# Mixing channels on four quarters of TensorE's array, and laying one stage's work between another's by time

## The chip, the cores and the metric

The kernel runs on one core of one Trainium2 chip. The metric is the device time of one execution in microseconds; the time of the kernel before is the median of three runs. All data are fp32. The engines are called as in the profile: PE is TensorE's matmul, PEld its weight load, DVE is VectorE, ACT is ScalarE, POOL is GpSimd, and SP is the queue that issues the transfers.

## The reference, cut to what matters

Four layers follow each other on a tensor of 4 images x 64 channels x 256 x 256. Layers 0, 2 and 3 are long convolutions in two dimensions with a separable filter, plus a bias times the input. Layer 1 works on Haar coefficients:

```python
def _L1_conv_ref(x, v, conv_w, tau):          # x: (4, 64, 256, 256)
    f1 = haar2d(x)
    acc = jnp.zeros_like(f1[:, :conv_w.shape[1]])
    for i in range(v.shape[0]):               # two terms, i = 0 and 1
        f3 = f1 * v[i]
        f4 = jnp.einsum('bchw,oc->bohw', f3, conv_w[i])      # mixes the 64 channels
        f5 = jnp.sign(f4) * jax.nn.relu(jnp.abs(f4) - tau[i])
        acc = acc + f5
    y = haar2d(acc, inverse=True)
    return y + x
# ... layers 0, 2, 3:  y = (2D convolution of x with hx * hy) + x * bias
```

v[i] and tau[i] have one value per pixel, and v is the same for all channels, so the kernel mixes first and multiplies by v afterwards.

## The kernel before

The batch is cut into two groups of two images. The kernel has three phases. A is layer 0 and the Haar transform, and writes the coefficients to DRAM (`coef`). B is the mixing of channels and the threshold, and writes `mixed`. C is the inverse transform with layers 2 and 3. B is laid beside the others: B of the first group beside A of the second, and B of the second group beside C. Each phase is a list of pieces, and `beside` says how many pieces of the one follow each piece of the other; an engine works through its instructions in the order in which the pieces emit them.

A round of A treats two channels of two images, and has 12 pieces: four of rows, four of columns and four of the product with the Haar matrix (M = 4). A round of C has 16.

```python
    def toeplitz(ps, data, t, which):                      # a row or column piece: 2 x this pair
        for m in range(2):
            cut = bass.ts(m, P)
            nc.tensor.matmul(ps[:, m, :], data[:, 0, cut], t[:, which, :], start=True, stop=False)
            nc.tensor.matmul(ps[:, m, HALF:], data[:, 1, cut], t[:, which, :HALF], start=False, stop=True)
# ... phase A, column piece: what VectorE does after it
            later(
                lambda: nc.vector.scalar_tensor_tensor(
                    s["x1"][:, cut], s["x"][:, cut], bias_sb[:, c : c + 1], ps, ALU.mult, ALU.add
                )
            )
# ... phase A, product piece
            for e in range(2):
                for k in range(2):
                    nc.tensor.matmul(
                        ps[:, e, bass.ts(k, P)],
                        s["fw"][:, 2 * (n + e) + k, bass.ts(m, P)],
                        haarH_sb[:, k, :],
                        start=True,
                        stop=True,
                    )
```

Phase B goes by rows of coefficients, 64 steps of two units each (P = 128, C = 64, N = 256, W = 512, NB = 2). In the first group ("not packed") 64 channels x 2 rows fill the partitions, and a unit is one of the two terms i. In the second group ("packed") a unit is one image, and the matrix holds both terms side by side: its 128 output columns are 64 channels of term 0 and 64 of term 1. The lower 64 partitions of the data hold one row, the upper 64 another; each half of the array's rows mixes its own.

```python
        def mix(u):
            f = st[u // 2]["f"]
            un[u]["f4"] = bps.tile([P, 2, W], F32, tag="f4", name=f"f4_{grp}_{u}")   # PSUM, two buffers
            if packed:
                for h in range(2):
                    cut = bass.ts(h, N)
                    for q in range(2):
                        rows = slice(q * C, (q + 1) * C)
                        nc.tensor.matmul(
                            un[u]["f4"][:, q, cut],
                            mixers[0][rows, 0],
                            f[rows, u % 2, cut],
                            start=True,
                            stop=True,
                            tile_position=(q * C, 0),
                        )
            else:
                for j in range(2):
                    nc.tensor.matmul(un[u]["f4"][:, j, :], mixers[0][:, u % 2, :], f[:, j, :], start=True, stop=True)
        def multiply(u):
            f4 = un[u]["f4"]
            nc.vector.tensor_tensor(f4, f4, weights(u, "v"), ALU.mult)
        # sign(u):      m  = sign(f4)              ScalarE
        # magnitude(u): f4 = abs(f4)               ScalarE
        # less(u):      f4 = f4 - tau              VectorE
        def threshold(u):
            nc.vector.scalar_tensor_tensor(un[u]["m"], un[u]["f4"], 0.0, un[u]["m"], ALU.max, ALU.mult)
# ...
        def sort(s, name, q):                              # packed only
            if q == 0:
                tag, bufs = ("gt", 3) if name == "g" else ("other", 2)
                st[s][name] = bp.tile([P, NB, W], F32, tag=tag, name=f"{tag}_{grp}_{s}", bufs=bufs)
            i = q if name == "g" else 1 - q
            src = st[s]["m"][i * C : (i + 1) * C, :, q]
            nc.scalar.copy(st[s][name][q * C : (q + 1) * C], src)

        def add_sorted(s, name):
            g = st[s]["g"]
            nc.gpsimd.tensor_tensor(g, g, st[s][name], ALU.add)
# ...
        def unit(u, j):
            if j == 0:
                if u < units:
                    mix(u)
                if 0 < u <= units:
                    less(u - 1)
            elif j == 1:
                if u < units:
                    multiply(u)
                    sign(u)
                if 0 < u <= units:
                    threshold(u - 1)
            elif u < units:
                magnitude(u)
```

In the packed result the partitions stand for the term and the free dimension for the row, while the output needs the row on the partitions and the sum of both terms. So four copies per step (`sort`) bring the parts to their places, into `g` and `other`, and two additions on GpSimd add the input and `other`.

```python

    def beside(main, side, lead, tail):

        done = 0
        for k, p in enumerate(main):
            p()
            want = len(side) * max(0, k + 1 - lead) // max(1, len(main) - lead - tail)
            for q in side[done:want]:
                q()
            done = max(done, want)
# ...
    beside(a[cut_a : -6 * M], phase_b(0, False), 5 * M, 0)       # A of group two, B of group one
# ...
    beside(main, phase_b(1, True), 5 * M, 0)                     # C, B of group two
```

Of the kernel before, what the change touches and what calls it, by code (L numbers as in the profile page):

```python
# [35 lines left out]
F32 = mybir.dt.float32  # L39
AF = mybir.ActivationFunctionType  # L40
ALU = mybir.AluOpType
# [3 lines left out]
P = 128  # L45
B, C, N = 4, 64, 256
# [10 lines left out]
COPIES = 8  # L57

GROUPS = 2
NB = B // GROUPS  # L60
CI = 4 // NB
M = CI * NB

ROUNDS = C // CI
STEPS = C
W = 2 * N
# [10 lines left out]
def conv_haar_kernel(  # L77
    ctx: ExitStack, tc: tile.TileContext, x, zT, w1, wbd, cols, decay, wo_first, decay_first, bias, haarW, haarH, ident, wcol, wrow, mixT, packT, v, v2, tau, out
):
    nc = tc.nc  # L80
# [11 lines left out]
    taus2 = dram.tile([C, 2, COPIES, 2, W], F32, tag="taus2", name="taus2")  # L92


    def pool(name, bufs, stack=ctx, **kw):
        return stack.enter_context(tc.tile_pool(name=name, bufs=bufs, reuse_waits="tile", **kw))
# [151 lines left out]
    def copy_tau(k):  # L248
        tau_sb = thresholds[1]
        for i in range(2):  # L250
            at = taus2.offset + (i * COPIES + k) * 2 * W
            to = bass.AP(taus2.tensor, at, [[4 * W * COPIES, C], [W, 2], [1, W]])
            nc.sync.dma_start(to, tau_sb[:, 2 * i : 2 * i + 2].rearrange("p h k -> p (h k)"))

    first_x = [load_x(0)]
# [19 lines left out]
    rest += [lambda l=l, q=q, k=k: spread(l, q, k) for l in (1, 2) for q in range(4) for k in thirds]  # L275
    rest.append(scale_tau)
    rest += [lambda k=k: copy_tau(k) for k in range(COPIES)]

    def toeplitz(ps, data, t, which):
# [238 lines left out]
    def phase_b(grp, packed):  # L518
# [3 lines left out]
        mixers = []  # L522
        st = [dict() for _ in range(STEPS)]
        un = [dict() for _ in range(units)]
        pieces = []

        def rows_of(ap, s):
            n = NB * W
            by_partition = [[n, P]] if packed else [[n, C], [C * n, 2]]
            return bass.AP(ap.tensor, ap.offset + 2 * s * C * n, by_partition + [[1, n]])  # L530

        def load(s):
            if s >= STEPS:
                return
            d = st[s]
            d["f"] = bp.tile([P, NB, W], F32, tag="ft", name=f"ft_{grp}_{s}", bufs=4)
            nc.sync.dma_start(d["f"].rearrange("p b w -> p (b w)"), rows_of(coef[grp], s))
            for name, src in (("v", v2), ("tau", taus2)) if packed else (("v", v), ("tau", taus)):
                t = d[name] = bp.tile([P, 2, W], F32, tag=name, name=f"{name}_{grp}_{s}", bufs=3)
                if packed:  # L540

                    at, by_partition = s * 4 * W * COPIES, [[2 * W, 2 * COPIES], [0, C // COPIES]]
                else:

                    at, by_partition = s * 4 * W, [[0, C], [2 * W, 2]]
                flat = bass.AP(src.tensor, src.offset + at, by_partition + [[1, 2 * W]])
                nc.sync.dma_start(t.rearrange("p e w -> p (e w)"), flat)
# [5 lines left out]
        def mix(u):  # L553
            f = st[u // 2]["f"]
            un[u]["f4"] = bps.tile([P, 2, W], F32, tag="f4", name=f"f4_{grp}_{u}")
            if packed:

                for h in range(2):
                    cut = bass.ts(h, N)
                    for q in range(2):  # L560
                        rows = slice(q * C, (q + 1) * C)
                        nc.tensor.matmul(  # L562
                            un[u]["f4"][:, q, cut],
                            mixers[0][rows, 0],
                            f[rows, u % 2, cut],
                            start=True,
                            stop=True,
                            tile_position=(q * C, 0),
                        )
            else:  # L570

                for j in range(2):
                    nc.tensor.matmul(un[u]["f4"][:, j, :], mixers[0][:, u % 2, :], f[:, j, :], start=True, stop=True)  # L573
# [29 lines left out]
                st[s]["g"] = bp.tile([P, NB, W], F32, tag="gt", name=f"gt_{grp}_{s}", bufs=3)  # L603
                nc.gpsimd.tensor_tensor(st[s]["g"], m0, un[2 * s + 1]["m"], ALU.add)

        def sort(s, name, q):

            if q == 0:
                tag, bufs = ("gt", 3) if name == "g" else ("other", 2)
                st[s][name] = bp.tile([P, NB, W], F32, tag=tag, name=f"{tag}_{grp}_{s}", bufs=bufs)  # L610
            i = q if name == "g" else 1 - q
            src = st[s]["m"][i * C : (i + 1) * C, :, q]
            nc.scalar.copy(st[s][name][q * C : (q + 1) * C], src)  # L613

        def add_sorted(s, name):
            g = st[s]["g"]
            nc.gpsimd.tensor_tensor(g, g, st[s][name], ALU.add)  # L617

        def store(s):
            nc.sync.dma_start(rows_of(mixed[grp], s), st[s]["g"].rearrange("p b w -> p (b w)"))  # L620
            st[s].clear()
# [15 lines that stand above are left out]
# [10 lines left out]
        def piece_packed(u, j):  # L647
            unit(u, j)
            s, i = divmod(u, 2)

            if j != 1:
                of = s - 1 if (i, j) != (0, 0) else s - 2
                name, q = {(0, 2): ("g", 0), (1, 0): ("g", 1), (1, 2): ("other", 0), (0, 0): ("other", 1)}[i, j]
                if 0 <= of < STEPS:
                    sort(of, name, q)
            if j == 1 and i and 1 <= s <= STEPS:
                add_sorted(s - 1, "f")
            if j == 1 and not i and 2 <= s <= STEPS + 1:
                add_sorted(s - 2, "other")
                store(s - 2)  # L660
            if j == 1 and not i and s >= 2:
                load(s + 2)

        def start():
# [183 lines left out]
        pieces.append(lambda: (flush(), store(total - 1)))  # L848
        return before, first, pieces

    def beside(main, side, lead, tail):

        done = 0
        for k, p in enumerate(main):
            p()
            want = len(side) * max(0, k + 1 - lead) // max(1, len(main) - lead - tail)
            for q in side[done:want]:
                q()
            done = max(done, want)

    (a, a_last), (c_before, c_first, c) = phase_a(), phase_c()
    cut_a, cut_c = ROUNDS * 3 * M, (ROUNDS - 2) * 4 * M
    beside(a[:cut_a], rest, 2, 3 * M)
    early.close()
    during = ctx.enter_context(ExitStack())
    bp = pool("b", 2, during)
    bps = pool("bps", 2, during, space=PSUM)

    beside(a[cut_a : -6 * M], phase_b(0, False), 5 * M, 0)
    beside(a[-6 * M : -2 * M], c_before[:1], 2 * M, M)  # L870
    beside(a[-2 * M :], c_before[1:], 0, 0)
    during.close()
    bp = pool("b2", 2, during)
    bps = pool("bps2", 2, during, space=PSUM)
    main = a_last[:1] + c_first + c[:M]
# [120 lines left out]
```

## Time and profile before

| | |
|---|---|
| median of 3 runs | 2817.47 us (2817.18 to 2818.97) |
| span of the profiled run | 2817.2 us, granted clock 0.999 |
| A of group one, with the filters' networks | 0 to 484 us |
| A of group two with B of group one | 484 to 1122 us |
| the change from A to C | 1122 to 1196 us |
| C with B of group two | 1196 to 2030 us |
| C alone | 2030 to 2817 us |
| mixing, group one (whole array) | 512 passes of 512 columns, busy 248 us |
| mixing, group two (row halves) | 1024 passes of 256 columns, busy 145 us |
| one multiply, subtraction or threshold of a unit on VectorE | 1.21 to 1.23 us |
| one copy of `sort` on ScalarE | 1.04 us, 256 of them |
| one addition of `add_sorted` on GpSimd | 2.36 us, 128 of them |

The boundaries of the stages were read from the first and last start of the mixing matmuls. Matmul records overlap, since their ends are modelled: a row that says how long one lasted is longer than the time that it takes from the next. Every fp32 matmul appears as two records, one per pass. PSUM tiles of B appear under the name `f`, as A's output does; the line number tells them apart (L562 and L573 are the two forms of the mixing). The line of a chain's row names the work that ended last before the next step of the chain could begin.

### The profile page before, as it was taken

How to read it: one execution, taken by the hardware profiler on the slowest of the kernel's cores; microseconds unless marked ns; L12 is line 12 of the kernel's file. 1: busy time of each engine (PE TensorE's matmuls, PEld its weight loads, DVE VectorE, ACT ScalarE, POOL GpSimd, SP SyncE). 2: the span in 40 equal slices, each digit the busy share in tenths (PEclk: the TensorE clock that was granted, in tenths of full speed). 3: DMA queues.
4: the chain of work that ended last, by engine and by line, in shares of the span. 5: the costliest groups of instructions: out<-in, count | busy, mean ns of one | idle time of the engine just before them, and what ended most of it. 6: DMA issues, size and time to landing. Idle time of an engine off the chain costs nothing.

```text
span 2817.2 us, 47099 instructions
## 1 busy us (share of the span) xinstructions
PE 2769.1 (98%) x16940; PEld 2406.2 (85%) x16940; DVE 1964.7 (70%) x3461; ACT 1394.6 (50%) x1987; POOL 1958.0 (70%) x2486
## 2 busy tenths in 40 slices
PE   7999999999999999999999999999999999999999
PEld 6989999777777777988888888888899999999998
DVE  3676663887888888378888888888755556666664
ACT  2344434555555555377777777777722221122211
POOL 4777777888888888867767777777774445555540
PEclk9999999999999999999999999999999999999999
DMA  7758877988888887599889899899654444444442
GB/s 210 225 188 263 260 255 253 339 325 317 321 321 321 321 321 276 199 278 292 263 259 277 265 275 267 267 268 271 197 163 147 145 146 137 137 139 135 135 138 81
DMA packets 237448, 661.92 MB, mean 235 GB/s; under 512 B 26622, under 2 KB 135711, under 8 KB 204704
## 3 DMA queue, kind: packets, MB, share of 16 engines
q1 hardware_dynamic: 237216, 658.90, 72.1%
q8 instruction: 136, 2.23, 0.3%
q14 instruction: 96, 0.79, 0.1%
HBM read 438.60 MB, written 220.20 MB: 234 GB/s over the span
## 4 chain that ended last, share of the span: by engine, by line
PE 85%; DVE 7%; issue 3%; ACT 2%; POOL 2%; DMA 1%; SPq 0%; DVEq 0%; ACTq 0%; POOLq 0%
PE c1r L283 8%; PE c2c L283 8%; PE c1c L283 8%; PE c2r L283 8%; PE a1ps L283 6%; PE a2ps L283 6%; PE f L573 5%; PE f L562 5%; PE c2c L284 4%; PE c1r L284 4%; PE c1c L284 4%; PE c2r L284 4%; PE a3ps L391 3%; PE a1ps L284 3%; PE a2ps L284 3%
## 5 line engine op out<-in xcount | busy, mean ns | idle before, releaser
L586 ACT ACTIVATE m<-f 128x1024 f32<-128x1024 f32 x256 | 262.6, 1026 | 428.7 <-DVE f L577 397.2
L593 DVE TENSOR_TENSOR f<-f,tau 128x1024 f32<-128x1024 f32 x256 | 314.7, 1229 | 165.5 <-ACT f L589 165.5
L577 DVE TENSOR_TENSOR f<-f,v 128x1024 f32<-128x1024 f32 x256 | 314.1, 1227 | 58.3 <-PE f L562 40.7
L283 PE MATMUL a1ps<-toep,x 128*128 128x256 f32 x1024 | 308.3, 383 | 3.2 <-DMA toep<-filt 3.2
L596 DVE SCALAR_TENSOR_TENSOR m<-f,m 128x1024 f32<-128x1024 f32 x256 | 310.6, 1213 | 0.0
L283 PE MATMUL c2r<-toep,cy 128*128 128x256 f32 x1024 | 309.1, 384 | 0.0
L283 PE MATMUL c2c<-toep,ch 128*128 128x256 f32 x1024 | 309.1, 384 | 0.0
L283 PE MATMUL c1c<-toep,ch 128*128 128x256 f32 x1024 | 309.1, 384 | 0.0
L771 ACT COPY ch<-c2r 128x512 f32<-128x512 f32 x256 | 149.4, 585 | 317.4 <-PE c2r L284 316.4
L283 PE MATMUL a2ps<-toep,ay 128*128 128x256 f32 x1024 | 305.7, 380 | 0.0
L771 ACT COPY ch<-c1r 128x512 f32<-128x512 f32 x256 | 149.2, 585 | 305.8 <-PE c1r L284 304.8
L573 PE MATMUL f<-ft,mix 128*128 128x512 f32 x512 | 248.2, 607 | 21.6 <-DVE m L596 20.9
L589 ACT ACTIVATE f<-f 128x1024 f32<-128x1024 f32 x256 | 262.8, 1027 | 0.0
L400 ACT ACTIVATE f<-a3ps,wcol_sb 128x512 f32<-128x512 f32 x196 | 131.7, 686 | 215.7 <-PE a3ps L391 210.1
L371 DVE SCALAR_TENSOR_TENSOR x<-x,bias_sb,a2ps 128x512 f32<-128x512 f32 x256 | 187.9, 742 | 70.6 <-PE a2ps L284 70.0
L318 POOL TENSOR_TENSOR i<-g 128x8 f32<-128x8 f32 x63 | 13.7, 217 | 317.2 <-DMA g<-mixed 317.1
L785 DVE SCALAR_TENSOR_TENSOR o<-cy,bias_sb,c2c 128x512 f32<-128x512 f32 x256 | 188.1, 740 | 65.1 <-PE c2c L284 64.8
L617 POOL TENSOR_TENSOR gt<-gt,ft 128x1024 f32<-128x1024 f32 x64 | 151.3, 2364 | 111.7 <-ACT gt L613 111.7
L318 POOL TENSOR_TENSOR i<-i,g 128x16 f32<-128x16 f32 x378 | 206.3, 546 | 25.9
L617 POOL TENSOR_TENSOR gt<-gt,other 128x1024 f32<-128x1024 f32 x64 | 151.4, 2365 | 100.0 <-ACT other L613 99.7
L284 PEld LDWEIGHTS a1ps<-toep,x 128*128 128x128 f32 x1024 | 195.9, 191 | 27.0
L284 PEld LDWEIGHTS a2ps<-toep,ay 128*128 128x128 f32 x1024 | 194.6, 190 | 26.3
(103 smaller groups left out, 7204.4 us busy)
## 6 DMA issues: line engine op xcount, KB each, us to landing
toep<-filt SPq DMA_DIRECT2D x768, 128.0 KB, 5.5
coef<-f SPq DMA_DIRECT2D x64, 1024.0 KB, 4.4
ft<-coef SPq DMA_DIRECT2D x128, 512.0 KB, 6.5
v<-in_v SPq DMA_DIRECT2D x128, 512.0 KB, 7.2
tau<-taus SPq DMA_DIRECT2D x128, 512.0 KB, 7.7
mixed<-gt SPq DMA_DIRECT2D x128, 512.0 KB, 4.3
g<-mixed SPq DMA_DIRECT2D x64, 1024.0 KB, 8.8
x<-in_x SPq DMA_DIRECT2D x63, 1024.0 KB, 8.5
```

Source lines behind the costliest of these rows:

```text
L283: nc.tensor.matmul(ps[:, m, :], data[:, 0, cut], t[:, which, :], start=True, stop=False)
L284: nc.tensor.matmul(ps[:, m, HALF:], data[:, 1, cut], t[:, which, :HALF], start=False, stop=True)
L318: engine.tensor_tensor(even, s, d, ALU.add)
L573: nc.tensor.matmul(un[u]["f4"][:, j, :], mixers[0][:, u % 2, :], f[:, j, :], start=True, stop=True)
L577: nc.vector.tensor_tensor(f4, f4, weights(u, "v"), ALU.mult)
L586: nc.scalar.activation(un[u]["m"], un[u]["f4"], AF.Sign)
L589: nc.scalar.activation(un[u]["f4"], un[u]["f4"], AF.Abs)
L593: nc.vector.tensor_tensor(f4, f4, weights(u, "tau"), ALU.subtract)
L596: nc.vector.scalar_tensor_tensor(un[u]["m"], un[u]["f4"], 0.0, un[u]["m"], ALU.max, ALU.mult)
L617: nc.gpsimd.tensor_tensor(g, g, st[s][name], ALU.add)
L771: later(lambda: nc.scalar.copy(y, ps))
L785: later(lambda: nc.vector.scalar_tensor_tensor(o, old, bias_sb[:, at : at + 1], ps, ALU.mult, ALU.add))
```

## The change: what it does and what it is for

Three things change. First, a packed unit is mixed by four matmuls that each use one quarter of the array (64 rows x 64 columns) over all 512 columns of data, instead of four that each use one half of the rows (64 x 128) over 256 columns. Each quarter makes one term of one row. The quarters are paired so that term 0 of the lower row comes out on the lower partitions and term 0 of the upper row on the upper ones, in the place where the output needs them; term 1 comes out with the two halves exchanged. v and tau are laid out in the same order beforehand. Then only term 1 has to change halves: two copies per step instead of four (`exchange`), and the first addition takes term 0 where it stands (`add_first`). It is for less work on ScalarE and a shorter way from mixing to store.

Second, those steps stand at other places among the pieces, and the store comes earlier.

Third, `beside` takes weights: B of the first group is laid between A's pieces in proportion to 13 for a row or column piece and 9 for a product piece, instead of evenly by number. It is for an even distance in time between B's pieces.

```diff
@@ -248,8 +249,10 @@
     def copy_tau(k):
         tau_sb = thresholds[1]
         for i in range(2):
-            at = taus2.offset + (i * COPIES + k) * 2 * W
-            to = bass.AP(taus2.tensor, at, [[4 * W * COPIES, C], [W, 2], [1, W]])
+            at, half = taus2.offset + (k * 2 + i) * W, 2 * W * COPIES
+            by_row = [[half, 2]] if i == 0 else [[-half, 2]]
+            to = bass.AP(taus2.tensor, at + i * half, [[2 * half, C]] + by_row + [[1, W]])
             nc.sync.dma_start(to, tau_sb[:, 2 * i : 2 * i + 2].rearrange("p h k -> p (h k)"))
 
     first_x = [load_x(0)]
@@ -555,17 +558,16 @@
             un[u]["f4"] = bps.tile([P, 2, W], F32, tag="f4", name=f"f4_{grp}_{u}")
             if packed:
 
-                for h in range(2):
-                    cut = bass.ts(h, N)
+                for i in range(2):
                     for q in range(2):
-                        rows = slice(q * C, (q + 1) * C)
+                        rows, half = slice(q * C, (q + 1) * C), (q + i) % 2 * C
                         nc.tensor.matmul(
-                            un[u]["f4"][:, q, cut],
-                            mixers[0][rows, 0],
-                            f[rows, u % 2, cut],
+                            un[u]["f4"][half : half + C, i, :],
+                            mixers[0][rows, 0, bass.ts(i, C)],
+                            f[rows, u % 2],
                             start=True,
                             stop=True,
-                            tile_position=(q * C, 0),
+                            tile_position=(q * C, half),
                         )
             else:
 
@@ -603,18 +605,19 @@
                 st[s]["g"] = bp.tile([P, NB, W], F32, tag="gt", name=f"gt_{grp}_{s}", bufs=3)
                 nc.gpsimd.tensor_tensor(st[s]["g"], m0, un[2 * s + 1]["m"], ALU.add)
 
-        def sort(s, name, q):
+        def exchange(s, q):
 
             if q == 0:
-                tag, bufs = ("gt", 3) if name == "g" else ("other", 2)
-                st[s][name] = bp.tile([P, NB, W], F32, tag=tag, name=f"{tag}_{grp}_{s}", bufs=bufs)
-            i = q if name == "g" else 1 - q
-            src = st[s]["m"][i * C : (i + 1) * C, :, q]
-            nc.scalar.copy(st[s][name][q * C : (q + 1) * C], src)
-        def add_sorted(s, name):
-            g = st[s]["g"]
-            nc.gpsimd.tensor_tensor(g, g, st[s][name], ALU.add)
+                st[s]["other"] = bp.tile([P, NB, W], F32, tag="other", name=f"other_{grp}_{s}", bufs=2)
+            src = st[s]["m"][(1 - q) * C : (2 - q) * C, :, 1]
+            nc.scalar.copy(st[s]["other"][q * C : (q + 1) * C], src)
+        def add_first(s):
+            st[s]["g"] = bp.tile([P, NB, W], F32, tag="gt", name=f"gt_{grp}_{s}", bufs=3)
+            nc.gpsimd.tensor_tensor(st[s]["g"], st[s]["m"][:, :, 0], st[s]["f"], ALU.add)
+        def add_second(s):
+            nc.gpsimd.tensor_tensor(st[s]["g"], st[s]["g"], st[s]["other"], ALU.add)
 
         def store(s):
             nc.sync.dma_start(rows_of(mixed[grp], s), st[s]["g"].rearrange("p b w -> p (b w)"))
@@ -648,17 +651,17 @@
             unit(u, j)
             s, i = divmod(u, 2)
 
-            if j != 1:
-                of = s - 1 if (i, j) != (0, 0) else s - 2
-                name, q = {(0, 2): ("g", 0), (1, 0): ("g", 1), (1, 2): ("other", 0), (0, 0): ("other", 1)}[i, j]
-                if 0 <= of < STEPS:
-                    sort(of, name, q)
-            if j == 1 and i and 1 <= s <= STEPS:
-                add_sorted(s - 1, "f")
-            if j == 1 and not i and 2 <= s <= STEPS + 1:
-                add_sorted(s - 2, "other")
-                store(s - 2)
-            if j == 1 and not i and s >= 2:
+            if 1 <= s <= STEPS:
+                if (i, j) == (0, 2):
+                    exchange(s - 1, 0)
+                    add_first(s - 1)
+                if (i, j) == (1, 0):
+                    exchange(s - 1, 1)
+                if (i, j) == (1, 1):
+                    add_second(s - 1)
+                if (i, j) == (1, 2):
+                    store(s - 1)
+            if (i, j) == (0, 1) and s >= 2:
                 load(s + 2)
 
         def start():
@@ -848,12 +851,15 @@
         pieces.append(lambda: (flush(), store(total - 1)))
         return before, first, pieces
 
-    def beside(main, side, lead, tail):
+    def beside(main, side, lead, tail, weights=(1,)):
+
+        weights = [weights[k % len(weights)] for k in range(len(main))]
+        all_of = sum(weights[lead : len(main) - tail])
         done = 0
         for k, p in enumerate(main):
             p()
-            want = len(side) * max(0, k + 1 - lead) // max(1, len(main) - lead - tail)
+            want = len(side) * sum(weights[lead : k + 1]) // max(1, all_of)
             for q in side[done:want]:
                 q()
             done = max(done, want)
@@ -866,7 +872,8 @@
     bp = pool("b", 2, during)
     bps = pool("bps", 2, during, space=PSUM)
 
-    beside(a[cut_a : -6 * M], phase_b(0, False), 5 * M, 0)
+    beside(a[cut_a : -6 * M], phase_b(0, False), 5 * M, 0, [13] * (2 * M) + [9] * M)
     beside(a[-6 * M : -2 * M], c_before[:1], 2 * M, M)
     beside(a[-2 * M :], c_before[1:], 0, 0)
     during.close()
@@ -944,6 +951,8 @@
 
     filters = [np.repeat([w * C + r * CI + e for w in range(2) for e in range(CI)], REPEATS) for r in range(FIRST)]
     wo = _blocks(a[CONV[0] + "Xwo"], a[CONV[0] + "Ywo"])
+    rows = by_row(v).reshape(C, 2, 2, W)
     arrays = {
 
         "x": f(a["x"].reshape(GROUPS, NB, C, 2, P, N).transpose(0, 4, 2, 1, 3, 5)),
@@ -979,7 +988,8 @@
         "mixT": f(mix.reshape(P, 2, P)),
         "packT": f(np.concatenate([pack, pack], axis=0)[:, None]),
         "v": by_row(v),
-        "v2": f(np.repeat(by_row(v).reshape(C, 2, 2, W).transpose(0, 2, 1, 3)[:, :, None], COPIES, axis=2)),
+        "v2": f(np.repeat(np.stack([rows[:, :, 0], rows[:, ::-1, 1]], axis=2)[:, :, None], COPIES, axis=2)),
         "tau": by_row(tau),
     }
     nc = bacc.Bacc("TRN2", target_bir_lowering=False, num_devices=1)
```

Blank lines that the change adds or removes are left out of the diff.

## The prediction

> **What bounds the kernel now.** I read the busy shares first, then TensorE's waits, then the four stages one by one, because the change touches only two of them. From the page of the kernel before, busy time by engine and the chain of work that ended last:
>
> ```profile
> PE 2769.1 (98%) x16940; PEld 2406.2 (85%) x16940; DVE 1964.7 (70%) x3461; ACT 1394.6 (50%) x1987; POOL 1958.0 (70%) x2486
> ...
> PE 85%; DVE 7%; issue 3%; ACT 2%; POOL 2%; DMA 1%; SPq 0%; DVEq 0%; ACTq 0%; POOLq 0%
> ```
>
> TensorE is the bound: 85% of the chain is matmuls one after another. So the other engines count only where TensorE waits for them. All its waits for DVE and POOL, from the view of waits:
>
> ```profile
> PE f L573 <- DVE m L596: 20.9, 38, 1.5
> ...
> PE c1ps L714 <- DVE ci L320: 2.3, 1, 2.3
> PE a3ps L391 <- DVE t L455: 1.4, 2, 1.0
> PE a3ps L391 <- POOL fw L297: 1.3, 2, 0.8
> ```
>
> Only one is of size: B's mixing matmul of group one (L573) waits 38 times, 20.9 us in all, for VectorE's threshold (L596) to release one of its two PSUM buffers. Now the two stages in which B runs, as windows: 484 to 1122 us is A of group two with B of group one, 1196 to 2030 us is C with B of group two (columns: window, its length, then busy us of each engine, clock, DMA share, GB/s):
>
> ```profile
> 484.00:1122.00 638.00, 616.39 (x3113) 461.19 (x3112) 513.62 (x488) 363.75 (x472) 558.79 (x641) 1.00 0.88 321
> ...
> 1196.00:2030.00 834.00, 833.18 (x5342) 720.73 (x5341) 676.45 (x835) 648.90 (x848) 612.51 (x579) 1.00 0.91 268
> ```
>
> In the first, TensorE is idle for 638.0 - 616.4 = 21.6 us. In the second it is idle for 0.8 of 834 us: there ScalarE (649 busy), VectorE and POOL have room, and no wait is left to remove. That stage changes only by TensorE's own work. What a unit of packed mixing costs there can be read from the chain, piece by piece (start, length, what):
>
> ```profile
> 1606.68 0.43 PE c1r L283 x2
> 1607.12 0.22 PE c1r L284 x2
> 1607.34 1.06 PE f L562 x8
> 1608.40 0.63 PE c1r L283 x2
> 1609.03 0.22 PE c1r L284 x2
> 1609.25 0.43 PE c1r L283 x2
> ```
>
> Each fp32 matmul shows as two passes, so a unit's four matmuls are x8. Eight passes of 256 columns at 0.216 us would be 1.73 us in a row; they take 1.06 us, because the two row halves of the array run side by side: the records of one unit start at 0, 0.007, 0.320, 0.327, 0.536, 0.543, 0.752 and 0.758 us, four pairs. The following pair of C's passes then takes 0.63 instead of 0.43. Over the 128 units I find 0.095 us before the first pass, 1.064 in it and 0.104 in the first whole-array pass after it, 1.26 us in all, 162 us for the stage. Four pairs are 0.866; the remaining 0.396 us (51 us for all units) is changing the array's shape and back.
>
> **What the Trainium skill says.** "TensorEngine Tiling (Array Packing)", Key Properties: changing the tiling mode drains TensorE, and tiles can load weights and multiply in parallel. The trace agrees with both: the 0.396 us, and the pairs 7 ns apart. The same page's Tiling Modes lists four 64x64 tiles, which is what the change uses; no run here shows four at once. "TensorE: Matmul & The Clock Gate", Measured speedup vs the span model, gives 2.38x for three column tiles and 10.6x for sixteen tiles, but not with fp32's two passes. Its Part 3, The mechanism, calls matmuls strict FIFO. The trace of before disagrees in one respect: the compiled program puts both passes of the first half ahead of those of the second, and yet the second half's first pass starts 7 ns after the first's, not after its second pass. So a half does not queue behind the other half; whether a quarter queues behind the other quarter of its own half is the open question. The same page, LDWEIGHTS, says that a weight load's time goes by its columns (columns/1.2 ns). 128 columns would be 107 ns, and the first pass of a unit is indeed 0.104 us longer (0.320 against 0.216); for 64 columns an estimate from that formula is 53 ns.
>
> **The change, part by part.**
>
> *Mixing of group two.* Removed: per unit four matmuls of 64 rows x 128 outputs x 256 columns. Added: four of 64 rows x 64 outputs x 512 columns. The array work is the same: two pass slots of 512 columns, which L573's passes show at 0.430 us each, so 0.859 against 0.866, if all four quarters run at once. The changes of shape stay, two per unit. The one gain I see is the weight load at the head of the unit: 64 columns a quarter, 0.05 us less if both quarters of a half load together, nothing if in turn. 128 x (0 to 0.05 + 0.007) = 1 to 7 us; I take 4.
>
> *One exchange copy per row.* ScalarE loses two of four copies per row: 128 of 256 at 1.04 us (L613), 133 of its 649 us. POOL keeps two adds of 2.36 us per row, but the first reads the product itself and no longer waits for a copy (POOL waited 211 us for L613). All of this is beside TensorE, which waited for none of it: 0 us. The store moves up by about a unit, also off the path. The new layouts of v and tau have the same sizes and counts of transfers: 0 us.
>
> *Laying B of group one by time.* The cost of a wait is how much later a mixing starts than the passes ahead of it allow. I summed this over the 128 units: 30.6 us (more than the view's 20.9, which counts idle time after the modelled ends). Of this 20.8 us lies behind A's product pieces (L391), 9.0 behind its row pieces and 0.8 behind its column pieces. The reason is in the durations: a row or column piece is 1.31 us of passes, a product piece 0.88, a mixing 1.72. B now comes every 2.56 pieces, whatever they are, so two mixings stand 3.5 to 5.6 us apart. But from one mixing to the release of the next buffer run the mixing (1.72), VectorE's multiply (1.23) and threshold (1.21): 4.2 us plus hand-overs. Waits begin where the distance is under about 4.4 us. With weights 13 and 9 (1.31 to 0.88 is 13 to 8.7) the short distances should go. Both compiled orders, with each pass at its traced time, give these counts; the loss is what the trace of before has for that class:
>
> - behind a product piece, 3.5 us apart: 12 mixings losing 11.8 us; 1 in the new order, 1.0
> - behind a product piece, 3.9: 6 losing 2.9; now 5, 2.4
> - behind a product piece, 4.35: 13 losing 4.6; now 13, 4.6
> - behind a product piece, more: 10 losing 1.6; now 13, 2.0
> - behind a row piece, 3.9: 4 losing 3.8; now 2, 1.9
> - behind a row piece, 4.3: 17 losing 5.1; now 22, 6.6
> - behind a column piece, 4.3: 17 losing 0.8; now 32, 1.5
> - all longer ones: 0.2 in both
>
> The sum goes from 30.6 to 20.2 us. A mixing that waited also has a longer first pass (0.53 against 0.45 us, 56 of them), which gives 1 to 2 us more. Against it stands VectorE: under the columns it also does A's adds (0.74 us each), and B now gets denser there, 1.305 instead of 1.17 of its pieces per column piece. At 3.67 us of VectorE a unit that is 2.34 us of VectorE for 2.05 of TensorE per column piece (before: 2.17 for 1.97), so the backlog after four columns grows from 0.8 to 1.2 us. I take 2 us off: 10 us gained.
>
> Sum: 2817.5 - 10 - 4 = 2803.5, say 2804.
>
> **Rivals.**
>
> *A quarter queues behind the other quarter of its half.* Each half would run first-first, second pass beside the other quarter's first, then that one's second: three slots for two, +0.43 us a unit, +55 us: 2859. For it: only independence of halves is seen in the trace. Against it: tiles are described as independent. I give it one in five.
>
> *Quarters that share rows don't run together at all* (both stream the same 64 partitions): four slots, +0.86 us x 128 = +110 us: about 2914. The stage has no idle time to swallow it. One in seven.
>
> *The waits of group one only move under the columns*: VectorE is busy 514 of 638 us there and POOL 559, and a smoother order doesn't take work from them. Then that part gives about nothing and the time is about 2813. For it: the thinner slack worked out above. Against it: the classes that disappear held 12 us.
>
> *ScalarE's relief speeds C up*: a gain only if TensorE waited for ScalarE, and it was idle 0.8 us. I give it nothing.
>
> **Range and chances.** If four quarters run together (about two in three), the time is 2797 to 2814, from 1 to 7 us and 3 to 13 us of gain. The three-slot case lies near 2859, the four-slot case near 2914. A range of 2793 to 2863 holds the first two. Faster by over 2% would need 56 us, more than all shape changes (51) and far above all waits: 0.01. Slower by over 2% is nearly the four-slot case alone: 0.14. Within 2%: 0.85.
>
> **What would show it.** In the changed profile the unit of mixing of group two should stay near 1.06 us in the chain, its records starting in two groups of four some 0.43 us apart; three or four groups make the first or second rival true and the C stage 55 or 110 us longer. The pair of C's passes after it should still take 0.63. ScalarE's copies there should halve, with TensorE's idle time in that stage still near 1 us. TensorE's wait for L596's threshold should fall from 20.9 to about 12 to 15 us, the rest behind row and column pieces; if it doesn't fall, the third rival holds. I would be wrong altogether if a fresh wait shows up in C, such as the sign (which now waits for POOL to read the product) holding up VectorE.

## The result, and the profile after

The changed kernel takes 2810.2 us (median of 4 runs, 2809.5 to 2810.8) against 2817.8 for the kernel before (also a median of 4): a ratio of 0.9972 (95% interval 0.9955 to 0.9990). That is 7.6 us, about half of the 14 predicted. Line numbers of the changed kernel are two or three higher: L575 is L573 of before (mixing, group one), L564 is L562 (group two), L598 the threshold.

Busy time and chain by engine:

```profile
PE 2763.1 (98%) x16940; PEld 2343.8 (83%) x16940; DVE 1964.7 (70%) x3461; ACT 1275.8 (45%) x1859; POOL 1955.6 (70%) x2486
...
PE 86%; DVE 5%; issue 3%; POOL 2%; ACT 2%; DMA 1%; SPq 0%; DVEq 0%; ACTq 0%; POOLq 0%
```

ScalarE lost 119 us and 128 instructions; TensorE bounds the kernel as before. Its waits, the ones that matter here:

```profile
PE f L575 <- DVE m L598: 11.2, 25, 1.1
...
PE f L575 <- PE a2ps L287: 5.0, 9, 1.0
...
PE c1ps L717 <- DVE ci L323: 2.3, 1, 2.3
PE a3ps L394 <- POOL fw L300: 2.0, 3, 0.8
PE a3ps L394 <- DVE t L458: 1.3, 2, 1.0
PE f L575 <- issue: 1.2, 1, 1.2
```

The view puts the wait for the threshold at 11.2 us where it was 20.9, but 5.0 us behind A's column matmuls (a2ps) and 1.2 us of "issue" are new for L575. They are the same wait under other names: each of these ten mixings starts 0.10 us after the end of a threshold, while what the view names had come 0.28 us or more before the start. So 17.4 us of waiting for the threshold are left. The chain through a packed unit in C:

```profile
1601.49 0.22 PE c1r L287 x2
1601.71 1.02 PE f L564 x8
1602.73 0.63 PE c1r L286 x2
1603.36 0.22 PE c1r L287 x2
```

1.02 us where it was 1.06, and still 0.63 for the pair behind. The eight records of a unit start at 0, 0.007, 0.013, 0.020 and 0.480, 0.487, 0.493, 0.500 us: two groups of four. All four quarters run together, and none queues behind the other quarter of its half. TensorE's idle time beside B of group two is 1.1 of 836 us (0.8 of 834 before).

Where the 7.6 us come from, from the two traces: the 128 packed units with their changes of shape take 155.8 instead of 161.6 us, 5.8 less. The late starts of group one's mixing (summed as in the prediction) fall from 30.6 to 27.8 us, 2.8 less: behind product pieces from 20.8 to 9.8, behind row pieces from 9.0 to 5.9, and behind column pieces they rise from 0.8 to 12.1.

### The profile page after: what moved, and what is told of

Its sections match the earlier page's. It is cut to its first block, busy times and chain, and to the rows that moved or that the text cites. A ratio compares the mean times of both kernels' runs of the same rounds, so it can differ in the third digit from the quotient of the medians.

```text
span 2809.0 us, 47062 instructions
## 1 busy us (share of the span) xinstructions
PE 2763.1 (98%) x16940; PEld 2343.8 (83%) x16940; DVE 1964.7 (70%) x3461; ACT 1275.8 (45%) x1859; POOL 1955.6 (70%) x2486
## 4 chain that ended last, share of the span: by engine, by line
PE 86%; DVE 5%; issue 3%; POOL 2%; ACT 2%; DMA 1%; SPq 0%; DVEq 0%; ACTq 0%; POOLq 0%
PE c2c L286 8%; PE c1r L286 8%; PE c1c L286 8%; PE c2r L286 8%; PE a1ps L286 6%; PE f L575 6%; PE a2ps L286 6%; PE f L564 5%; PE c2c L287 4%; PE c1c L287 4%; PE c2r L287 4%; PE c1r L287 4%; PE a3ps L394 4%; PE a1ps L287 3%; PE a2ps L287 3%
## 5 line engine op out<-in xcount | busy, mean ns | idle before, releaser
L588 ACT ACTIVATE m<-f 128x1024 f32<-128x1024 f32 x256 | 262.3, 1024 | 495.5 <-DVE f L579 468.2
L598 DVE SCALAR_TENSOR_TENSOR m<-f,m 128x1024 f32<-128x1024 f32 x256 | 311.1, 1215 | 0.0
L617 POOL TENSOR_TENSOR gt<-m,ft 128x1024 f32<-128x1024 f32 x64 | 151.4, 2365 | 180.2 <-DVE m L598 180.1
L575 PE MATMUL f<-ft,mix 128*128 128x512 f32 x512 | 248.4, 608 | 18.4 <-DVE m L598 11.2
L374 DVE SCALAR_TENSOR_TENSOR x<-x,bias_sb,a2ps 128x512 f32<-128x512 f32 x256 | 188.1, 742 | 69.5 <-PE a2ps L287 59.7
L403 ACT ACTIVATE f<-a3ps,wcol_sb 128x512 f32<-128x512 f32 x196 | 130.7, 686 | 217.8 <-PE a3ps L394 206.6
L287 PEld LDWEIGHTS c1c<-toep,ch 128*128 128x128 f32 x1024 | 194.6, 190 | 26.3
```

The lines of the kernel that those rows point to most:

```text
L374: lambda: nc.vector.scalar_tensor_tensor(s["x1"][:, cut], s["x"][:, cut], bias_sb[:, c : c + 1], ps, ALU.mult, ALU.add)
L588: nc.scalar.activation(un[u]["m"], un[u]["f4"], AF.Sign)
```

## The experiments

**The two parts one at a time.** First the changed kernel with even spacing:

```diff
-    beside(a[cut_a : -6 * M], phase_b(0, False), 5 * M, 0, [13] * (2 * M) + [9] * M)
+    beside(a[cut_a : -6 * M], phase_b(0, False), 5 * M, 0)
```

> The changed kernel with B of the first group laid evenly by number again, so that only the quarters and the single exchange remain of the change. Theory (the two parts are independent, and the quarters' gain is TensorE's own work, 0.045 us a unit as the changed kernel's trace shows): the mixing unit of group two stays at 1.02 us, TensorE's waits for the threshold in group one go back to about 21 us, and the time is about 2812 us (5.8 below before). Rival (the gain came mostly from the weights): about 2816.

2812.8 us, 0.9985 of before (0.9978 to 0.9991). The unit is 1.019 us, the wait for the threshold 21.0 (from the profiled execution, the longest of 21 with 2817.6 us). Then the kernel before with the weights alone:

```diff
-    def beside(main, side, lead, tail):
+    def beside(main, side, lead, tail, weights=(1,)):       # body as in the change
-    beside(a[cut_a : -6 * M], phase_b(0, False), 5 * M, 0)
+    beside(a[cut_a : -6 * M], phase_b(0, False), 5 * M, 0, [13] * (2 * M) + [9] * M)
```

> The kernel before with nothing but the weights 13 and 9. Theory (late starts of group one fall from 30.6 to 27.8 us, because waits behind product pieces go but new ones come behind column pieces): about 2815 us, 2 to 3 below before. Rival (the 10 us of the prediction are there, and something else in the changed kernel took part of them back): about 2807.

2814.9 us, 0.9991 (0.9983 to 1.0000), with the late starts of the changed kernel to within 0.1 us. Together the parts give 4.46 + 2.35 = 6.8 of the 7.6 us, the same within the intervals. The quarters gave what was forecast; the weights gave a quarter of it.

**What the quarters save.** The kernel before with two packed matmuls per unit of 512 columns on the row halves:

```diff
-                for h in range(2):
-                    cut = bass.ts(h, N)
-                    for q in range(2):
-                        rows = slice(q * C, (q + 1) * C)
-                        nc.tensor.matmul(un[u]["f4"][:, q, cut], mixers[0][rows, 0], f[rows, u % 2, cut], ...)
+                for q in range(2):
+                    rows = slice(q * C, (q + 1) * C)
+                    nc.tensor.matmul(un[u]["f4"][:, q, :], mixers[0][rows, 0], f[rows, u % 2], ...)
```

> The kernel before with the packed mixing as two matmuls per unit of 64 rows x 128 outputs x 512 columns (row halves) instead of four of 256 columns. It tells what the quarters' 0.045 us a unit is. Theory (the load of 64 instead of 128 weight columns at the head of the unit): with 128 columns loaded as before the unit stays at about 1.055 us and the time at about 2817. Rival (two pass slots instead of four, fewer instructions): the unit falls to about 1.02 us and the time to about 2812.

2817.0 us, ratio 1.0000 (0.9992 to 1.0008), and in its chain:

```profile
1606.10 1.06 PE f L560 x4
1607.15 0.63 PE c1r L283 x2
```

The starts are 0, 0.007, 0.533 and 0.540 us: the first slot is 0.104 longer than its 0.430, as with 256 columns, while with quarters it is 0.050 longer (0.480). So half as many slots save 0.005 us, which rules out the count of slots. The other 0.054 us at the head of the unit go with the weight load: its next load starts 0.108 us after the first on the halves and 0.055 us after it on the quarters. The stagger of four quarters takes some of it back. (Halves and quarters with the same number of weight columns were not compared.)

**Is ScalarE's relief worth anything?** Each exchange copy made twice, in one place:

```diff
-            nc.scalar.copy(st[s]["other"][q * C : (q + 1) * C], src)
+            for _ in range(2):
+                nc.scalar.copy(st[s]["other"][q * C : (q + 1) * C], src)
```

> The changed kernel with each exchange copy made twice, into the same place, so that ScalarE does as many copies beside C as in the kernel before (133 us more busy) and the result is the same. Theory (ScalarE's relief is worth nothing, TensorE waits for no copy): 2810 us, unchanged. Rival (part of the gain is ScalarE's): 2812 to 2816.

2849.1 us: 39 us slower than the changed kernel, further off than either theory. TensorE, which had waited 0.4 us for C's copies, now waits 15 us for them, above all here:

```profile
PE c1ps L718 <- ACT ch L775: 8.1, 10, 1.4
...
PE c2r L286 <- ACT ch L775: 4.5, 5, 1.3
```

and ScalarE's order of time shows how:

```profile
1600.93 1.02 ACT L591 ACTIVATE f<-f 128x1024 f32<-128x1024 f32 x1
1601.98 2.12 ACT L614 COPY other<-m 64x1024 f32<-64x1024 f32 x2
1604.01 0.57 ACT L775 COPY ch<-c2r 128x512 f32<-128x512 f32 x1
```

C's copy of a finished product stands behind 2.1 us of B's copies. The rest of the 39 us is not accounted for; the doubled copies also delay B itself (GpSimd waits 107 us for `other`, 25 in the changed kernel). This tests a clump as well as a load, so the two extra copies were put where the kernel before had its third and fourth:

```diff
+        def again(s, q):                 # at (1, 2) of the same row and (0, 0) of the next
+            if s >= 1:
+                src = kept[s]["m"][(1 - q) * C : (2 - q) * C, :, 1]
+                nc.scalar.copy(kept[s - 1]["other"][q * C : (q + 1) * C], src)
```

> The changed kernel with two more copies per row on ScalarE at the places where the kernel before had its third and fourth (they write into a buffer that is dead, so the result is the same). ScalarE's load beside C is that of the kernel before again, without two copies in one place. Theory (the 39 us of the run with doubled copies came from 2.1 us of ScalarE in one place, behind which C's own copies stood; the number of copies as such costs nothing): 2810 us, unchanged. Rival (the load itself costs, and ScalarE's relief is part of the change's gain): 2813 to 2850.

2810.4 us: unchanged. The two extra copies cost nothing in these places; doubled in one place they cost 39 us.

**Why the weights gave so little.** The first theory was a loop through TensorE: mixing, multiply, threshold, next mixing. The swap takes the mixing out of it:

```diff
             elif j == 1:
+                if not packed and 0 < u <= units:
+                    threshold(u - 1)
                 if u < units:
                     multiply(u)
                     sign(u)
-                if 0 < u <= units:
+                if packed and 0 < u <= units:
                     threshold(u - 1)
```

> The changed kernel with VectorE's threshold of the unit before standing ahead of the multiply of the unit (group one only). Theory (the waits come from a loop: the multiply waits for the mixing to end, the threshold stands behind the multiply, and the next mixing waits for the threshold, so 1.72 + 1.23 + 1.21 us and hand-overs lie between two mixings; the swap takes the mixing and the multiply out of that loop): late starts fall from 27.8 to under 10 us, TensorE's idle time in group one from 18 to under 6 us, and the time is about 2792 us. Rival (VectorE is simply behind under the column pieces, 2.34 us of it for 2.05 of TensorE): the waits stay, 2805 to 2812.

2954.5 us, 144 us slower than the changed kernel. The theory fell, and the trace of the changed kernel shows what had been overlooked. VectorE and then ScalarE in order of time (the bracket: idle before it, and what ended it):

```profile
690.29 1.23 DVE L595 TENSOR_TENSOR f<-f,tau 128x1024 f32<-128x1024 f32 x1 [1.46 <-ACT f L591]
691.43 1.22 DVE L579 TENSOR_TENSOR f<-f,v 128x1024 f32<-128x1024 f32 x1
692.56 1.22 DVE L598 SCALAR_TENSOR_TENSOR m<-f,m 128x1024 f32<-128x1024 f32 x1
695.29 1.23 DVE L595 TENSOR_TENSOR f<-f,tau 128x1024 f32<-128x1024 f32 x1 [1.52 <-ACT f L591]
696.43 1.22 DVE L579 TENSOR_TENSOR f<-f,v 128x1024 f32<-128x1024 f32 x1
```

```profile
692.74 1.03 ACT L588 ACTIVATE m<-f 128x1024 f32<-128x1024 f32 x1 [1.31 <-POOL gt L606]
693.66 0.68 ACT L403 ACTIVATE f<-a3ps,wcol_sb 128x512 f32<-128x512 f32 x1
694.23 1.03 ACT L591 ACTIVATE f<-f 128x1024 f32<-128x1024 f32 x1
695.17 0.60 ACT L363 COPY ay<-a1ps 128x512 f32<-128x512 f32 x1
```

From one multiply (691.43) to the next (696.43) run multiply, sign, a scaling of A's (L403), magnitude and subtraction: 5.00 us in which each waits for the one before (the bracket at L588 names an addition on GpSimd that ended 0.06 us after the multiply), while TensorE's passes alone put two mixings 4.8 us apart on average. This is a second loop, between VectorE and ScalarE. The threshold stood in its shadow, beside ScalarE; the swap put it in the line:

```profile
703.63 1.22 DVE L579 TENSOR_TENSOR f<-f,v 128x1024 f32<-128x1024 f32 x1
707.43 1.23 DVE L595 TENSOR_TENSOR f<-f,tau 128x1024 f32<-128x1024 f32 x1 [2.58 <-ACT f L591]
708.70 1.22 DVE L598 SCALAR_TENSOR_TENSOR m<-f,m 128x1024 f32<-128x1024 f32 x1
709.84 1.22 DVE L579 TENSOR_TENSOR f<-f,v 128x1024 f32<-128x1024 f32 x1
```

The mean distance from multiply to multiply in group one goes from 4.99 to 6.12 us, 1.13 more, which is one threshold; 144 us over 127 units is the same.

If so, what shortens this loop must help. Magnitude first, sign second, so that the subtraction waits for one ScalarE operation only (it then reads the SBUF tile m):

```diff
-            nc.scalar.activation(un[u]["m"], un[u]["f4"], AF.Sign)
+            nc.scalar.activation(un[u]["m"], un[u]["f4"], AF.Sign if packed else AF.Abs)
-            nc.scalar.activation(un[u]["f4"], un[u]["f4"], AF.Abs)
+            nc.scalar.activation(un[u]["f4"], un[u]["f4"], AF.Abs if packed else AF.Sign)
-            nc.vector.tensor_tensor(f4, f4, weights(u, "tau"), ALU.subtract)
+            size = un[u]["f4" if packed else "m"]
+            nc.vector.tensor_tensor(size, size, weights(u, "tau"), ALU.subtract)
+            # threshold: max(size, 0) times the other tile, into m
```

> The changed kernel with the order on ScalarE turned round in group one: the magnitude is taken first (into the SBUF tile m), the sign second (in place in PSUM), so that VectorE's subtraction of tau waits for one ScalarE operation and not for two. The order on VectorE stays. New theory (the pace of group one is set by a loop between VectorE and ScalarE: multiply 1.23, sign and magnitude about 0.92 each with, at times, 0.57 of A's ScalarE work between them, subtraction 1.14 before the next multiply, 4.3 to 4.95 us for a distance of 4.7; the swap put 1.14 us more into it and gave 144 us / 127 = 1.13 us a unit): the loop falls to about 3.4 us, late starts of the mixing from 27.8 to under 12 us, and the time to about 2795 us. Rival (VectorE's work under the column pieces is the limit, whatever the order): 2806 to 2812.

2875.9 us, a miss of 80. The groups of this run between 484 and 1180 us, and its waits:

```profile
L595 DVE TENSOR_TENSOR m<-m,tau 128x1024 f32<-128x1024 f32 x127 | 248.5, 1957 | 2.5 <-ACT m L588 1.4
...
L295 POOL TENSOR_TENSOR fw<-f 128x256 f32<-128x256 f32 (+6 forms) x189 | 131.5, 696 | 9.8
```

```profile
PE a3ps L394 <- POOL fw L300: 46.2, 16, 5.6
PE f L575 <- DVE m L600: 20.6, 22, 1.7
```

The subtraction hardly waits for ScalarE any more (2.5 us instead of 110), but takes 1957 ns instead of 1232, and GpSimd's steps take longer too (696 against 426), so that A waits for GpSimd. It runs anywhere from 1208 to 3393 ns. The Trainium skill says why in "SBUF — State Buffer", section SBUF: two separate sides: a VectorE operation with two SBUF inputs and a GpSimd operation that reads SBUF exclude each other. The trace agrees with it: 85 of the 128 subtractions begin with more than 0.2 us of a GpSimd operation still to run, and each takes 1.21 us plus that rest, less 0.12 to 0.13 us; unhindered it is as fast as from PSUM. So the edit shortened the loop and broke something else; it doesn't decide. Nor does the same edit with the swap added:

> Magnitude first and, besides, the threshold ahead of the next multiply. Loop theory: the loop is multiply 1.23, magnitude 0.92, subtraction 1.14, threshold 1.13, 4.4 us, while the mixing has left it; with one more operation of VectorE in the loop than in the run with magnitude first alone it should be no better than that one, 2795 to 2803 us, and far from the 2954 us of the swap alone. Rival (the swap is slow for a reason of its own, not the ScalarE operations in the loop): above 2900 us.

2891.2 us, again with a slow subtraction (1.86 us on average): less than the swap alone, as the loop theory says, and far above its 2795 to 2803. The clean edit moves no operand, only A's work out of the loop. The magnitude is issued right behind the sign:

```diff
                     multiply(u)
                     sign(u)
+                    if not packed:
+                        magnitude(u)
...
-            elif u < units:
+            elif u < units and packed:
                 magnitude(u)
```

> The changed kernel with the magnitude issued right behind the sign in group one, so that no ScalarE work of A stands between them. Loop theory: 0.57 us leaves the loop in the units where A's copy or scaling stood there (about 4.9 becomes 4.3 us), late starts from 27.8 to about 15 us, time about 2798 us. Rival (VectorE's work is the limit): 2806 to 2812.

2799.7 us, 0.9934 of before (0.9921 to 0.9946), 10.5 us under the changed kernel. Late starts fall by as much, from 27.8 to 17.2 us: behind row pieces from 5.9 to 1.1, behind column pieces from 12.1 to 6.6. Behind product pieces they stay (9.8 and 9.5).

What holds up a late mixing can be read from VectorE's work just before the multiply of the unit ahead. In the changed kernel the subtraction there had waited for ScalarE ahead of 43 late starts, which lose 19.7 us; with the magnitude moved up it is 22 starts and 9.2 us. All others together keep theirs, 7.8 and 7.4 us. The first loop, through TensorE, in which the multiply waits for its own mixing, stands ahead of 4 late starts of the changed kernel, 2.1 us, all behind product pieces (8 and 4.9 us in the kernel before). Ahead of most others behind product pieces, 12 of 21 with 6.9 us, one of A's additions (L374) stands between the subtraction and the multiply:

```profile
494.73 1.23 DVE L595 TENSOR_TENSOR f<-f,tau 128x1024 f32<-128x1024 f32 x1
495.87 0.74 DVE L374 SCALAR_TENSOR_TENSOR x<-x,bias_sb,a2ps 128x512 f32<-128x512 f32 x1
496.52 1.23 DVE L579 TENSOR_TENSOR f<-f,v 128x1024 f32<-128x1024 f32 x1
497.66 1.22 DVE L598 SCALAR_TENSOR_TENSOR m<-f,m 128x1024 f32<-128x1024 f32 x1
```

A multiply that waits for nothing but its mixing starts 1.92 us after the mixing does; this one starts 2.96 us after it (mixing at 493.56), and the next mixing comes 0.45 us late, at 498.93. The same holds for 10 of the 18 behind column pieces, 8.8 us; there the subtraction had waited for ScalarE as well. No run takes A's additions out of the way, so their share is read and not tested.

With this edit the spacing can be tested again. Even spacing:

> The kernel with sign and magnitude adjacent, and B laid evenly by number. It tells what the weights are worth once the loop over ScalarE is short. Theory (behind column and row pieces the loop over ScalarE sets the waits, behind product pieces the loop mixing, multiply, threshold, which is untouched, 4.43 us): with product distances of 3.5 and 3.9 us back, late starts behind product pieces go from 9.5 to about 19 us, those behind columns from 6.6 to about 1, and the time is about 2803 us. Rival (the weights are worth nothing): 2800.

2802.6 us. Late starts behind product pieces are 19.0 us (about 19 expected) and behind column pieces 0.1 (about 1 expected). The 19 was forecast from the loop through TensorE, but the multiply waits for its mixing ahead of only 5.8 us of them: the number came true for other reasons too. So even spacing loses behind the product pieces, and 13 to 9 loses part of that gain under the columns, where VectorE also has A's adds. The next edit lays B thinner under the columns and denser under the rows:

```diff
-    ... phase_b(0, False), 5 * M, 0, [13] * (2 * M) + [9] * M)
+    ... phase_b(0, False), 5 * M, 0, [14] * M + [10] * M + [9] * M)
```

> Sign and magnitude adjacent, and weights 14 for row, 10 for column and 9 for product pieces, so that B is thinner where VectorE also does A's adds. Theory (what is left behind column pieces, 6.6 us, is VectorE's backlog from those adds; behind row pieces a distance of 4.33 us costs 0.01 us now, so there is room): late starts from 17.2 to about 11 us, time about 2794 us. Rival (VectorE stays behind whatever the placement): 2799 or more.

2789.6 us, 0.9895 of before (0.9880 to 0.9910), more than expected, which beats both kernels: 20.6 us under the changed one, 28.9 under the one before. In its waits the threshold is down to

```profile
PE f L575 <- DVE m L598: 2.3, 8, 0.6
```

and late starts are 8.3 us in all, 2.2 of them behind column pieces. The account closes to within 1 us: 30.6 - 8.3 = 22.3, and 5.8 for the quarters, is 28.1.

## Why the prediction was right or wrong

- *TensorE bounds, C with B has no wait to remove*: right. That stage shortened only by TensorE's own work.
- *Four quarters at once, 4 us (1 to 7) from the weight load*: right. 5.8 us by the trace, 4.5 by the run with this part alone; the run with 512 columns on halves shows that it is not the count of slots, and the starts of the loads, 0.108 and 0.055 us apart, speak for the load. Both rivals about queues and shared rows fell with the first record times.
- *ScalarE's relief is worth 0*: right (2810.4 with the copies back). The doubled copies show the limit of the argument: that TensorE waited for none of ScalarE's work held for copies spread out.
- *Laying by time, 10 us*: wrong in size, 2.8 by late starts and 2.4 in the run with it alone. One line of the sum failed: "behind a column piece, 4.3: 17 losing 0.8; now 32, 1.5". Those 32 lost 12.1. The other classes came to 15.7 us where 18.7 were forecast. The loss of a class was taken as belonging to the distance, but under the columns it depends on what came before. In the kernel before all 17 followed a distance over 5 us. Of the 32, 14 still do and lose 0.3 us; 18 follow another short one and lose 11.7 (6.5 with the magnitude moved up). The prediction saw a backlog of VectorE growing there, but took off 2 us for it. And the wait for the threshold that it wanted to see fall to 12 to 15 us reads 11.2 in the view, but is 17.4 with the ten starts under other names.
- *The cause given for the waits* (mixing, multiply, threshold, 4.2 us and hand-overs) was the smaller part: by VectorE's work ahead of them, 4.9 of the 30.6 us of late starts in the kernel before, all behind product pieces, while 15.0 us had a subtraction ahead that had waited for ScalarE. The loop multiply, sign, magnitude, subtraction, up to 5.0 us with a piece of A's on ScalarE in it, was not seen, although VectorE sat idle for 114.6 us before the subtractions of group one, waiting for ScalarE; that it cost time is shown by the run with the magnitude moved up. A's additions between subtraction and multiply are the third part, read from the trace alone. The third rival (waits move under the columns) came nearest, but not for its reason: VectorE's total work left room for 20 us more.
- The time of 2810.2 lies in the range of 2793 to 2863, which was wide upward for the sake of two rivals that did not come true.

## What to carry to other kernels

Before spacing work by time, write down every loop among the engines of one unit, with each operation of another stage that stands in it by accident of issue order, and compare it with the distance wanted; the longest loop sets the pace, and an engine with idle time can be in it. A loss read per distance does not carry over to another order if losses build up from one unit to the next. When two dependent operations of one engine lie on such a loop, issue them side by side: here this gave 10.5 us, where the change under study gave 7.6.

## What the runs showed of the hardware that was not expected

- The first passes of four 64x64 quarters start 7 ns apart, and the second passes 7 ns apart from 0.48 us on, although each quarter is one matmul of the kernel with two passes. No quarter's first pass waited for the second pass of the matmul issued before it.
- A VectorE subtraction takes 1.23 us with its data in PSUM, and 1.96 us on average (1.21 to 3.39) with both inputs in SBUF beside a busy GpSimd, whose own steps lengthen too. The run that moved this operand lost 66 us against the changed kernel, although it had one operation fewer in the loop.
